# Attention output by half batches, and the first context tokens prepared in the last self-attention batch

## The chip, the cores and the metric

The program runs on one core of one Trainium2 chip. The core has five engines with a queue of instructions each, worked off in order: TensorE (PE, with weight loads shown apart as PEld), VectorE (DVE), ScalarE (ACT), GpSimd (POOL) and SyncE (SP, here used for issuing DMA transfers). The engines wait for each other by semaphores. The metric is the device time of one execution in microseconds (us); lower is better. A profile is one execution taken by the hardware profiler; its span is the time from the first to the last instruction.

## The reference, cut to what matters

Four transformer blocks are chained over x of shape (4, 1024, 288), with a context of (4, 64, 288). Blocks 0 and 3 (`L0`, `L3`) are the same network with different weights, and the change concerns these two:

```python
h = layer_norm(x, ln1_g, ln1_b, 1e-06)
q8, s, sm = quant_act(h)           # rounded to -127..127, one scale per token
q, k, v = (quant_linear(q8, s, sm, w, b) for w, b in ...)      # 8-bit weights
a = attn(q, k, v)                  # 16 heads of 18, 1024 x 1024
a8, sa, sma = quant_act(a)
x = x + quant_linear(a8, sa, sma, wo1, bo1)
h = layer_norm(x, ln2_g, ln2_b, 1e-05)
q8, s, sm = quant_act(h)
q = quant_linear(q8, s, sm, wq2, bq2)
a = attn(q, cond @ wk2.T + bk2, cond @ wv2.T + bv2, mask)      # 64 context tokens
a8, sa, sma = quant_act(a)
x = x + quant_linear(a8, sa, sma, wo2, bo2)
h = quant_linear(quant_act(layer_norm(x, ln3_g, ln3_b, 1e-05)), wfc1, bfc1)
return x + quant_linear(quant_act(gelu(h)), wfc2, bfc2)        # 288 -> 1152 -> 288
```

Block 1 (`L1`, called vip in the kernel) is a cross-attention with two sets of keys, without norm or rounding; block 2 (`L2`) is another quantised transformer block. In blocks 0 and 3 only self-attention mixes the tokens of x, and only those of one batch: every other step can be taken for a few tokens by themselves as soon as their x is there.

## The kernel before, in words

x stays in SBUF for the whole program as 32 tiles of 128 tokens by 288 channels, eight tiles (`NTB`) to each of the four batches (`B`). The 16 heads are taken in four groups (`NG`). Block 0 and block 3 are each one call of `quant_net`; block 0's call also weaves block 1 into its last stage; block 2 is another function, which the change does not touch.

`quant_net` first calls `quant_self`, the self-attention. Its main loop runs over batch, head group, half of the queries (512 tokens) and key tile: 256 steps, each with four score products (line 2021), two exponentials (line 2031) and, one step behind, four products of exponentials and values (`weigh`, line 1981). All other work is woven in by `step()`, called once per loop step: it takes one piece (one `yield` of a Python generator) from the list `side`, in whose generators the operands of the next head group and the norms, roundings and values of the next batch stand, and if `side` is empty one from `spare`, which prepares the 8-bit weights of the later stages in 85 pieces and stores them in HBM. When the eight query halves and groups of a batch are done, `turn_heads` divides by the softmax sums (`heads_done`, lines 1936 to 1954) and appends `output(b)` to `side`: it rounds two tiles at a time (`round_levels`, lines 1414 to 1422), turns them (`turn_levels`, lines 1434 and 1437), multiplies them by wo1 and adds the result to x (`level_residual`: product in line 277, then lines 1755 and 1757 on DVE and line 1758 on POOL). For the last batch all of this comes after the loop: the last `weigh`, the rest of `spare`, then what is in `side`.

After that `quant_net` lays out SBUF and PSUM anew for the stage that follows. `ctx_stage` gives eight generators of four tiles each, the context attention: norm of x (`norm_apply`: line 1401 on ACT, 1404 and 1405 on POOL), rounding (`levels`: lines 1324 to 1333, turned in line 1349, copied in line 1354), the scales of the tokens spread over all partitions (`scale_cols`, line 2346; `over_tokens`, product in line 2358, copy in line 2363), query product (line 2212), attention, wo2 and its bias (line 1762). `ff_stage` gives 32 generators of one tile, the feed-forward. In block 0 `vip_aside` makes block 1's keys and values (loads in lines 2521 and 2527, products in line 2536, memsets in line 2567) and `vip_tokens` applies them. `run_stages` is a planner: from figures of cost that each generator yields it fixes the order in which the pieces are issued; a scheduler then orders each engine's queue and puts in the waits. Instructions of one engine are never overtaken at run time, and a transfer is issued on SP's or POOL's queue, in order, and waits there for its memory to be free. `tc.tile_pool` gives rotating buffers: with `bufs=1` the next tile of the same tag waits until all readers of the last one are done.

## Time and profile before

| | us |
|---|---|
| median of 3 runs | 4948.09 (4947.86 to 4956.46) |
| profiled execution | 4945.58 |
| its span | 4943.8 |
| PE busy in the span | 4245.7 (86%) |
| ACT busy | 3092.6 (63%) |
| DVE busy | 2986.6 (60%) |
| POOL busy | 1292.3 (26%) |
| last attention product of block 0 ends | at 785.5 |
| first context query product of block 0 starts | at 834.5 |
| last attention product of block 3 ends | at 4468.1 |
| first context query product of block 3 starts | at 4527.2 |

Busy time is the sum over an engine's instructions; the shares of different engines overlap. "Granted clock" is the share of TensorE's full rate that the chip's throttle allowed; its mean over this span was 0.848. A row `DVE amx L1324 <- POOL h L1405` among the waits says that DVE's instruction of line 1324, which writes amx, waited for POOL's of line 1405, which writes h.

### The profile page before, as it was taken

The numbers are of one execution on the slowest core, as the hardware profiler recorded it, in microseconds if no ns is written. First come the engines' busy times: TensorE is split into PE (matmuls) and PEld (weight loads), VectorE is DVE, ScalarE is ACT, GpSimd is POOL, SyncE is SP. The second block draws the span as 40 slices with busy tenths as digits, with TensorE's granted clock in tenths as the row PEclk, the third lists the DMA queues.
The fourth block names the chain that finished last, engine by engine and source line by source line (L and its number), as shares of the span: only waits on it lengthen the run. The fifth ranks groups of instructions, "written<-read, shape, count | busy, mean of one in ns | idle before, by whom it ended". The sixth has DMA issues, their size and how long they took to land. (4 is left out here: it accounts for less than half of the span.)

```text
span 4943.8 us, 63809 instructions
## 1 busy us (share of the span) xinstructions
PE 4245.7 (86%) x23291; PEld 1727.7 (35%) x23291; DVE 2986.6 (60%) x6645; ACT 3092.6 (63%) x4379; POOL 1292.3 (26%) x1934
## 2 busy tenths in 40 slices
PE   4999997888899979998888863899998999996676
PEld 2233323455565411110233331445543333322343
DVE  8454254665564589999788878433235455344775
ACT  3776774666662279998888853212114777774796
POOL 1001003443312576420112224111111010004664
PEclk9999998898999955555698885899998999997898
DMA  2000003100001221000000022001000000011000
GB/s 82 4 5 15 15 19 87 47 5 17 3 13 44 114 67 36 26 6 0 22 27 25 22 95 77 24 7 34 1 1 16 7 4 12 16 22 34 12 17 21
DMA packets 137702, 135.99 MB, mean 28 GB/s; under 512 B 69276, under 2 KB 114973, under 8 KB 135713
## 3 DMA queue, kind: packets, MB, share of 16 engines
q1 hardware_dynamic: 136176, 128.13, 8.6%
q0 software_dynamic: 1200, 3.69, 0.3%
q8 instruction: 185, 3.03, 0.3%
q14 instruction: 141, 1.15, 0.1%
HBM read 79.92 MB, written 43.47 MB: 25 GB/s over the span
## 5 line engine op out<-in xcount | busy, mean ns | idle before, releaser
L2031 ACT ACTIVATE e<-ps 128x1024 f32<-128x1024 f32 x1024 | 992.6, 1021 | 381.4 <-PE ps L2021 370.2
L2021 PE MATMUL ps<-qT,kT 32*128 32x512 f32 x4096 | 624.0, 644 | 4.1 <-DVE a L1943 3.9
L3025 DVE TENSOR_REDUCE top<-e 128x2 f32<-128x2048 f32 x256 | 563.5, 2274 | 14.2 <-ACT e L3018 14.0
L1981 PE MATMUL ps<-e,v 128*32 128x512 f32 x4096 | 549.4, 607 | 12.5 <-DVE oT L1992 12.5
L3394 PE MATMUL ps<-qk 32*128 32x512 bf16 x1024 | 499.9, 604 | 40.7 <-ACT e L3018 38.9
L3443 ACT ACTIVATE e<-ps 128x1024 f32<-128x1024 f32 x512 | 483.6, 1055 | 76.9 <-PE ps L3434 58.5
L3018 ACT ACTIVATE e<-ps 128x1024 f32<-128x1024 f32 x512 | 520.5, 1153 | 6.7 <-PE ps L3394 3.3
L1758 POOL TENSOR_TENSOR x<-x,y 128x288 f32<-128x288 f32 x192 | 153.2, 809 | 832.1 <-DVE y L1757 491.2
L3446 DVE TENSOR_SCALAR eb<-e 128x2048 bf16<-128x2048 f32 x256 | 321.7, 1260 | 47.7 <-ACT e L3443 45.5
L1404 POOL TENSOR_TENSOR h<-h,g 128x288 f32<-128x288 f32 x176 | 141.5, 808 | 507.2 <-ACT h L1401 474.5
L3434 PE MATMUL ps<-qk,kz 64*128 64x512 bf16 x1024 | 229.5, 445 | 41.9 <-ACT e L3443 37.8
L2021 PEld LDWEIGHTS ps<-qT,kT 32*128 32x128 f32 x4096 | 188.2, 184 | 208.4 <-issue 118.6
L2463 PE MATMUL psf<-hT,w 128*128 128x512 f32 x576 | 257.8, 600 | 0.6 <-ACT hT L2455 0.6
L1981 PEld LDWEIGHTS ps<-e,v 128*32 128x32 f32 x4096 | 81.0, 108 | 406.5 <-issue 347.1
L1349 PE MATMUL ps<-idb,q 128*128 128x128 bf16 (+2 forms) x1152 | 113.1, 243 | 126.3 <-ACT q L1333 72.7
L3394 PEld LDWEIGHTS <-qk 32*128 32x128 bf16 x1024 | 53.0, 99 | 465.1 <-issue 464.2
L3343 ACT ACTIVATE gl<-psf,bf 128x512 f32<-128x512 f32 x72 | 46.0, 684 | 269.0 <-PE psf L2467 264.8
L1354 ACT COPY qT<-ps 98x384 bf16<-98x384 bf16 (+3 forms) x256 | 151.7, 642 | 72.2 <-PE ps L1349 72.0
L277 PEld LDWEIGHTS <-qT 98*128 98x128 bf16 (+2 forms) x1344 | 134.6, 104 | 128.0 <-issue 41.3
L3347 DVE SCALAR_TENSOR_TENSOR u<-psf,bf,gl 128x512 f32<-128x512 f32 x72 | 51.1, 746 | 211.9 <-ACT gl L3343 211.9
L1880 POOL TENSOR_TENSOR v<-y,wv1b 128x288 f32<-128x288 f32 x64 | 51.7, 813 | 476.6 <-DVE y L1877 476.6
L3018 ACT ACTIVATION_READ_ACCUMULATOR e<-ps 128x1 f32 x512 | 172.9, 338 | 0.0
(506 smaller groups left out, 7803.0 us busy)
## 6 DMA issues: line engine op xcount, KB each, us to landing
raw<-y SPq DMA_DIRECT2D x32, 432.0 KB
in<-raw SPq DMA_DIRECT2D x30, 432.0 KB
kz<-qk SPq DMA_DIRECT2D x128, 64.0 KB
wn<-in_L_wfc SPq DMA_DIRECT2D x12, 432.0 KB
x<-in_x SPq DMA_DIRECT2D x4, 1152.0 KB
vvo<-vt SPq DMA_DIRECT2D x16, 288.0 KB
vo<-vvo SPq DMA_DIRECT2D x4, 1152.0 KB
rawq<-y SPq DMA_DIRECT2D x32, 144.0 KB
```

Source lines behind the costliest of these rows:

```text
L1354: nc.scalar.copy(qT[:, c0 : c0 + r, j0 * P : (j0 + per) * P].rearrange("p c (a t) -> p a c t", a=per), ps[:width, : per * r * P].rearrange ...
L1758: nc.gpsimd.tensor_tensor(self.x[:, t, :], self.x[:, t, :], y, ALU.add)
L1981: nc.tensor.matmul(acc[i * HP : (i + 1) * HP, :], lhsT=st["v"][:, kt, h * (D + 1) : h * (D + 1) + HP], rhs=es_[i // 2][:, i % 2, :], start ...
L2021: nc.tensor.matmul(pss[i // 2][:, i % 2, :], lhsT=self.row_tile(kT, i)[:, kt * P : (kt + 1) * P], rhs=self.row_tile(qT, i)[:, qh * 512 : ( ...
L2031: nc.scalar.activation(e, ps, AF.Exp, scale=SCALE)
L2463: nc.tensor.matmul(o, lhsT=lhs(i)[:, c, :], rhs=rhs(i)[:, c, :], start=(c == 0), stop=False)
L3018: nc.scalar.activation(e[:, j, :].rearrange("p (a n) -> p a n", a=2), sc, AF.Exp, scale=rstep, accum_out=sums[:, t, h0 + j : h0 + j + 1],)
L3025: nc.vector.tensor_reduce(top[:, t, h0 : h0 + 2], e, AX.X, ALU.max)
L3394: self.last = self.nc.tensor.matmul(ps[:, c, :], lhsT=self.row_tile(qT, i)[:, g, qt * P : (qt + 1) * P], rhs=self.row_tile(kT, i)[:, g, c ...
L3434: nc.tensor.matmul(pss[i][:, n, :], lhsT=kz[rows, i, kt * P : (kt + 1) * P], rhs=qT[rows, g, qh * 512 : (qh + 1) * 512], start=True, stop= ...
L3443: nc.scalar.activation(e[:, 2 * n : 2 * n + 2, :], ps, AF.Exp, scale=step)
L3446: nc.vector.tensor_scalar(eb, e, MAGIC, MAGIC, ALU.add, ALU.subtract)
```

## The change

- The output of self-attention is made in two halves of four tiles. The first half is appended to `side` as soon as the first query half of the last head group is done, the second after the other. The attention result `a` is now two tiles of a pool of its own (`halves`).
- A new generator `early` is appended to `side` during the last batch. It takes the norm statistics of batches 0 and 1 for the context stage, and normalises, rounds and turns the first four tiles into a buffer that outlives self-attention (`hT0`), with their scales (`srep0`). The norm uses DVE for all three operations (`norm_dve`), the scale columns too. The generator of the first context tokens takes these as they are.
- ln2's gain and bias (`g2`, `b2`) are loaded ahead of self-attention's.
- The pools of the last stage are laid in another order; context attention and feed-forward get separate work pools, so separate buffers of the same tag (`y`, two each). Fewer buffers are given to the rounded values `q` (x: 2; y: one less, and at most 4), to `oT` and `aT` (1), to the feed-forward's `h` (at most 5) and to `t` in `vip_aside` (1). In `vip_tokens` xT becomes a part of qT.

The diff, cut to its core:

```diff
         nc.vector.reciprocal(rs, sc)
-        q = self.wk.tile([P, m, n + terms], BF16, tag=f"q{tag}", name="q", bufs=bufs)
+        qb = {"x": 2, "y": max(2, min(bufs - 1, 4))}.get(tag, bufs)
+        q = self.wk.tile([P, m, n + terms], BF16, tag=f"q{tag}", name="q", bufs=qb)
...
+    def norm_stats_slow(self, t0, m, eps):
...
             nc.vector.bn_aggr(mv[:, j, :], st[:, j, :])
+            if j % 4 == 3:
+                yield
...
         return rstd, nmr
+
+    def norm_dve(self, h, t, stats, j, g, beta):
+
+        nc = self.nc
+        rstd, nmr = stats
+        nc.vector.tensor_scalar(
+            h, self.x[:, t, :], rstd[:, j : j + 1], nmr[:, j : j + 1], ALU.mult, ALU.add
+        )
+        nc.vector.tensor_tensor(h, h, g, ALU.mult)
+        nc.vector.tensor_tensor(h, h, beta, ALU.add)
...
         self.mm(ps[:, :C], qT[:, :, j * P : (j + 1) * P], w["T"], 0, C)
-        y = self.tmp(C, "y")
+        y = self.wk.tile([P, C], F32, tag="y", name="y", bufs=2)
...
             pool = lambda name, bufs: es.enter_context(tc.tile_pool(name=name, bufs=bufs))
-            wp, at = pool(f"{L}aw", 1), pool(f"{L}at", 2)
+            wp = pool(f"{L}aw", 1)
...
                     wo = self.level_weight(wp, np_, [(w["wo1"], w["bo1"])], C, CK, "wo1")
-            ep = pool(f"{L}ep", 5)
+            halves = pool(f"{L}ah", 3)
             es.enter_context(self.work(f"{L}ak"))
+            at, ep = pool(f"{L}at", 2), pool(f"{L}ep", 5)
...
-            def output(b):
-                a = state[b]["a"]
+            def output(b, hf):
+                a = state[b]["a"][hf]
                 now = None
-                for j in range(0, NTB + 2, 2):
+                for j in range(0, 4 + 2, 2):
                     ahead = None
-                    if j < NTB:
+                    if j < 4:
                         ahead = self.round_levels(a[:, j : j + 2, :], "o")
                     if now:
                         q, sc = now
-                        aT = self.wk.tile([CK, NC3, 2 * P], BF16, tag="qTo", name="aT")
+                        aT = self.wk.tile([CK, NC3, 2 * P], BF16, tag="qTo", name="aT", bufs=1)
                         self.turn_levels(q, CK, aT)
                     yield
                     if now:
                         for n in range(2):
-                            self.level_residual(aT, sc, wo, b * NTB + j - 2 + n, n, wo["b"])
+                            t = b * NTB + hf * 4 + j - 2 + n
+                            self.level_residual(aT, sc, wo, t, n, wo["b"])
                             yield
                     now = ahead
-                del state[b]
...
                 nc.vector.tensor_tensor(
-                    state[b]["a"][:, qh * 4 : qh * 4 + 4, g * 72 : (g + 1) * 72].rearrange(
+                    state[b]["a"][qh][:, :, g * 72 : (g + 1) * 72].rearrange(
...
                 if kt == NTB - 1:
-                    o = self.tmp(512, "oT")
+                    o = self.wk.tile([P, 512], F32, tag="oT", name="oT", bufs=1)
                     nc.vector.tensor_copy(o, acc)
                     done.append((b, g, qh, o))
             def turn_heads():
                 b, g, qh, o = done.pop()
                 heads_done(b, g, qh, o)
-                if (g, qh) == (NG - 1, 1):
-                    side.append(output(b))
+                if g == NG - 1:
+                    side.append(output(b, qh))
             run(levels(0))
             run(operands(0, 0))
             run(values(0))
             for b in range(B):
-                state[b]["a"] = at.tile([P, NTB, C], F32, tag="a", name="a")
+                state[b]["a"] = [
+                    halves.tile([P, 4, C], F32, tag="a", name="a") for _ in range(2)
+                ]
...
                         side.append(values(b + 1))
+                    elif g == 1:
+                        side.append(early())
...
-            self.quant_self(L, w, beside, ready)
+            g2 = self.load_bc(wp, w["ln2_g"], C, "g2")
+            b2 = self.load_bc(wp, w["ln2_b"], C, "b2")
+            made = {
+                "hT": wp.tile([CK, NC3, 512], BF16, name="hT0"),
+                "srep": wp.tile([P, 512], F32, name="srep0"),
+            }
+
+            def early():
+
+                for b in range(2):
+                    made[b] = yield from self.norm_stats_slow(b * NTB, NTB, 1e-5)
+                qs = []
+                for k in range(2):
+                    h = self.wk.tile([P, 2, C], F32, tag="h", name="h")
+                    for n in range(2):
+                        t = 2 * k + n
+                        self.norm_dve(h[:, n, :], t, made[0], t, g2, b2)
+                    yield
+                    qs.append(self.round_levels(h, "i"))
+                    yield
+                for k, (q, sc) in enumerate(qs):
+                    cols = slice(k * 2 * P, (k + 1) * 2 * P)
+                    self.turn_levels(q, CK, made["hT"][:, :, cols])
+                    scols = self.scale_cols(sc)
+                    yield
+                    self.over_tokens(sc, made["srep"][:, cols], scols)
+                    yield
+
+            self.quant_self(L, w, beside, ready, early)
             fp = pool(f"{L}fw")
-            g2 = self.load_bc(fp, w["ln2_g"], C, "g2")
-            b2 = self.load_bc(fp, w["ln2_b"], C, "b2")
             for k, v in (("sw", cw["swo"]), ("b", w["bo2"])):
                 cw["wo"][k] = fp.tile([P, C], F32, name=f"wo2{k}")
                 nc.sync.dma_start(cw["wo"][k], v.partition_broadcast(P))
             nb, m, nf = (2, 1, 3) if vip else (3, 1, 6)
-            cp = pool(f"{L}cb")
-            ctx = self.ctx_stage(cw, g2, b2, cp, nb)
-            first = next(ctx)
             g3 = self.load_bc(fp, w["ln3_g"], C, "g3")
             b3 = self.load_bc(fp, w["ln3_b"], C, "b3")
             w1 = self.stored_weight(fp, fw["T1"], fw["sw1"], None, "wfc1")
             w2 = self.stored_weight(fp, fw["T2"], fw["sw2"], w["bfc2"], "wfc2")
             rext = fp.tile([P, 2, 2 * B], F32, name="rext")
             tops = fp.tile([P, NT], F32, name="tops")
-            ctx_gens = [first] + [next(ctx) for _ in range(2 * B - 1)]
             cw["ext"] = rext
+            es.enter_context(self.work(f"{L}rf", 1))
+            ff_work = self.wk
             ff_gens = self.ff_stage(g3, b3, w1, w2, tops, out, m, nf)
-            stages = [
-                (ff_gens, nf, lambda i, d: i * m // 4 in d[1], None),
-                (ctx_gens, nb, lambda i, d: True, None),
-            ]
...
                 }
-                self.pb = pool(f"{L}pq", 4, space=PSUM)
+            cp = pool(f"{L}cb")
+            self.pb = pb = pool(f"{L}pq", 4 if vip else 8, space=PSUM)
+            stages = [
+                (ff_gens, nf, lambda i, d: i * m // 4 in d[1], lambda: (pb, ff_work)),
+                (list(self.ctx_stage(cw, g2, b2, cp, nb, made)), nb, lambda i, d: True, None),
+            ]
+            if vip:
                 vb = pool(f"{L}pv", 4, space=PSUM)
-                es.enter_context(self.work(f"{L}rk"))
+            es.enter_context(self.work(f"{L}rk"))
+            if vip:
...
                 ]
-            else:
-                self.pb = pool(f"{L}p", 8, space=PSUM)
-                es.enter_context(self.work(f"{L}rk"))
...
-    def ctx_stage(self, cw, g2, b2, pool, nb):
+    def ctx_stage(self, cw, g2, b2, pool, nb, made):
         nc = self.nc
         wq, wo, kb = cw["wq"], cw["wo"], cw["kb"]
-        keys, stats, there = {}, {}, {}
+        keys, there = {}, {0: 0, 1: 0}
+        stats = {b: made[b] for b in there}
...
             t0 = b * NTB + hf * 4
-            if hf == 0:
+            if hf == 0 and b not in there:
                 stats[b] = self.norm_stats(b, 1e-5)
                 there[b] = yield "d8.5", None, SIDE
             while b not in there:
                 yield "x1", None, SIDE
-            h = self.wk.tile([P, 4, C], F32, tag="h", name="h", bufs=nb)
-            for j in range(4):
-                self.norm_apply(h[:, j, :], t0 + j, stats[b], g2, b2)
-                if j % 2:
-                    yield "a1.1&g3.2", 0 if j == 1 else None, SIDE
-            hT, sc = yield from self.levels(h, None, CK, "x", 0, nb, SIDE)
-            srep = self.wk.tile([P, 512], F32, tag="srep", name="srep", bufs=nb)
-            for j in (0, 2):
-                two = sc[:, j : j + 2]
-                cols = self.scale_cols(two, nc.gpsimd)
-                yield "g.9", None
-                self.over_tokens(two, srep[:, j * P : (j + 2) * P], cols)
-                yield "p.5&a.4", 0 if j == 0 else None, SIDE
+            if t0 == 0:
+                hT, srep = made["hT"], made["srep"]
+            else:
+                h = self.wk.tile([P, 4, C], F32, tag="h", name="h", bufs=nb)
+                for j in range(4):
+                    self.norm_apply(h[:, j, :], t0 + j, stats[b], g2, b2)
+                    if j % 2:
+                        yield "a1.1&g3.2", 0 if j == 1 else None, SIDE
+                hT, sc = yield from self.levels(h, None, CK, "x", 0, nb, SIDE)
+                srep = self.wk.tile([P, 512], F32, tag="srep", name="srep", bufs=nb)
+                for j in (0, 2):
+                    two = sc[:, j : j + 2]
+                    cols = self.scale_cols(two, nc.gpsimd)
+                    yield "g.9", None
+                    self.over_tokens(two, srep[:, j * P : (j + 2) * P], cols)
+                    yield "p.5&a.4", 0 if j == 0 else None, SIDE
...
                 yield "x1", None, SIDE
-            h = self.wk.tile([P, m, C], F32, tag="fh", name="h", bufs=nb)
+            h = self.wk.tile([P, m, C], F32, tag="fh", name="h", bufs=min(nb, 5))
...
                 ahead = loads(g + 1)
-            ts = [np_.tile([P, B, 2 * T], F32, tag=f"t{n}", name=f"t{n}") for n in range(3)]
+            ts = [
+                np_.tile([P, B, 2 * T], F32, tag=f"t{n}", name=f"t{n}", bufs=1) for n in range(3)
+            ]
...
         b, n, w = t0 // NTB, t0 // 2, 2 * P
-        xT = self.wk.tile([P, 3, w], F32, tag="xT", name="xT")
+        qT = self.wk.tile([P, NG, w], F32, tag="qT", name="qT")
+        xT = qT[:, :3, :]
         for j in range(2):
             self.width_T(xT[:, :, j * P : (j + 1) * P], x[:, t0 + j, :])
             yield "p.9 a.5", 0 if j == 0 else None
-        qT = self.wk.tile([P, NG, w], F32, tag="qT", name="qT")
...
                 )
-        r = xT[:, 0, :]
+        r = qT[:, 0, :]
         nc.vector.reciprocal(r, ps)
         yield "p.9 d1.8", None
         pss = [self.ps1() for _ in range(4)]
```

More of the change, by code (lines that the diff above doesn't have):

```diff
@@ L1369, in norm_stats_of @@
     def norm_stats_of(self, t0, m, eps):
+        try:
+            at = self.norm_stats_slow(t0, m, eps)
+            while True:
+                next(at)
+        except StopIteration as end:
+            return end.value
+    def norm_stats_slow(self, t0, m, eps):
         nc = self.nc
@@ L1773, in psum_attn, with quant_self @@
             yield
-    def quant_self(self, L, w, beside, ready):
+    def quant_self(self, L, w, beside, ready, early):
         tc, nc = self.tc, self.nc
@@ L1835, in norms @@
                             continue
-                        j = 2 * k + n
-                        nc.vector.tensor_scalar(
-                            hn, self.x[:, t, :], stats[0][:, j : j + 1], stats[1][:, j : j + 1],
-                            ALU.mult, ALU.add,
-                        )
-                        nc.vector.tensor_tensor(hn, hn, g1, ALU.mult)
-                        nc.vector.tensor_tensor(hn, hn, b1, ALU.add)
+                        self.norm_dve(hn, t, stats, 2 * k + n, g1, b1)
                 for k in range(2):
```

## The prediction

> **What bounds the kernel now.** I read four views: busy time by stretches of the span, the timeline around the end of self-attention, the waits in that stretch, and the costliest groups. First the stretches, for block 0 and then block 3: the loop of self-attention, the gap from its last attention matmul to the first context query product (line 2212), and the stage of context attention and feed-forward. Columns: stretch, its length, busy us of PE, PEld, DVE, ACT, POOL, granted clock, DMA share, GB/s.
>
> ```profile
> 85.00:785.50 700.50, 684.07 (x4947) 210.59 (x4947) 322.99 (x956) 514.59 (x548) 57.63 (x107) 0.99 0.04 11
> 785.50:834.50 49.00, 14.59 (x87) 9.86 (x88) 25.82 (x60) 14.72 (x27) 36.70 (x59) 0.58 0.48 133
> 834.50:1570.00 735.50, 645.12 (x3941) 407.19 (x3940) 427.65 (x1307) 423.46 (x711) 231.35 (x427) 0.91 0.07 21
> 3768.80:4468.10 699.30, 685.40 (x4947) 210.72 (x4948) 318.43 (x908) 514.78 (x548) 57.09 (x106) 0.99 0.04 11
> 4468.10:4527.20 59.10, 18.75 (x103) 12.93 (x102) 29.75 (x61) 19.84 (x37) 42.60 (x58) 0.54 0.20 62
> 4527.20:4940.00 412.80, 302.81 (x1746) 162.82 (x1744) 279.99 (x985) 309.13 (x493) 221.83 (x403) 0.85 0.05 16
> ```
>
> In both loops PE is busy for 98% of the time: they are bound by TensorE, and DVE (46%), ACT (73%) and POOL (8%) have room. In the two gaps, 49.0 and 59.1 us, PE works for 14.6 and 18.8 us. They are latency: one chain of small operations through all engines. Block 0's is seen here in order of time (start, duration, engine; in brackets the idle time before and its releaser):
>
> ```profile
> 782.51 2.98 PE L1981 MATMUL ps<-e,v 128*32 128x512 f32 x16
> 800.72 1.69 POOL L1758 TENSOR_TENSOR x<-x,y 128x288 f32<-128x288 f32 x2 [1.51 <-DVE y L1757]
> 802.44 1.15 ACT L1401 ACTIVATE h<-x,nmr,rstd 128x288 f32<-128x288 f32 x2 [4.46 <-POOL x L1758]
> 810.24 1.53 POOL L1404 TENSOR_TENSOR h<-h,g 128x288 f32<-128x288 f32 x2 [2.90 <-DMA g<-in_L_ln_g]
> 816.30 1.35 DVE L1324 TENSOR_REDUCE amx<-h 128x4 f32<-128x1152 f32 x1 [13.22 <-POOL h L1405]
> 829.79 0.80 PE L2358 MATMUL ps<-idf,scol 128*128 128x128 f32 x2 [4.95 <-POOL scol L2346]
> 834.49 0.63 PE L2212 MATMUL ps<-qT,wq2T 96*128 96x512 bf16 x1
> ```
>
> The last attention matmul ends at 785.5; the eight tiles of the last batch's output reach x by 802.4; then x of the first batch, complete long ago, is normalised (ACT, POOL), rounded, turned and scaled, and only at 834.5 does the first query product start. The gain 2.9 us before 810.24 is a wait for the gain's load. The waits of the two gaps (waiting, releaser: total, times, longest) say the same of both blocks:
>
> ```profile
> PE ps L1349 <- ACT q L1333: 16.7, 3, 16.2
> DVE amx L1324 <- POOL h L1405: 13.9, 2, 13.2
> PE ps L2358 <- POOL scol L2346: 7.9, 3, 4.9
> ```
>
> ```profile
> PEld L1349 <- POOL h L1405: 21.1, 1, 21.1
> DVE amx L1324 <- POOL h L1405: 20.7, 3, 15.5
> PE ps L1349 <- POOL h L1405: 20.6, 1, 20.6
> ```
>
> **Removed: the chain of the first context tokens, from both gaps.** Its input is ready during the loop, and `early()` does it there, so after the change the first query product stands on PE directly behind the last output product. The gap shrinks to the tail of the output. Of that the first half (four tiles) also goes into the loop, but the rest is a chain: copy and turn of the last heads (785.5 to 787.8 before), then two pairs of tiles, which before reached x 3.1 to 4.4 us apart (787.8 is followed by a rounding of some 2.8 us, a turn, a copy and products of 3 us, and a second pair 4.1 us later). That is about 12 us.
>
> **Added to that tail: weight preparation.** Counting the 256 steps of the loop, the side work used 159 and left 97 for the 85 pieces of weight preparation; with early (12 pieces) and more output it leaves 76, so 9 pieces, part of wfc2, come after the loop: 5 roundings of 0.406 and 7 copies of 0.308 on DVE, 4.2 us, which is where the tail's chain also runs, and their stores. Tail: 12 + 4.2 = 16 to 17; I take 16.5.
>
> **Moved into the loop.** PE is full there, so its share is paid in full: transposes of two pairs (0.54 each) and four output products (0.45) for the output half, 2.9; two turns (0.54) and two scale spreads (0.66) for early, 2.4; less seven groups of weight transposes (0.3) that leave, 2.1: +3.2 us a block. On DVE early brings 16 statistics of 0.62, 12 norm operations of 0.45, two roundings of about 2.2 and the scale columns (no row on DVE: between 0.1, the least operation here, and POOL's 0.60 each; I take 0.6, four of them), 22 us, and the output half 7 us; the cover is DVE's 377 idle us in the loop, and without it all 29 would be paid. ACT gets four copies of 0.8 and two of 0.37, 3.9 us, against 186 idle; POOL four x updates of 0.81.
>
> Here a rule speaks against the change. DVE's two-input sums (line 1757) took 0.82 for two with POOL idle and 0.81 for two at 796.59, with POOL's selects running: no slowing. The Trainium skill, "SBUF — State Buffer", section "Who interferes with whom", says that a DVE operation with two SBUF inputs and a GpSimd operation that reads SBUF shut each other out for the whole instruction. By the row the eight new sums of g2 and b2 cost 8 x 0.45; by the rule each may also wait for a POOL operation of up to 0.81, 6.5 us in all. DVE has 377 us to lose: nothing on the path either way.
>
> **Block 0's sum.** 49.0 - 16.5 - 3.2 = 29.3 us earlier. Not all of it lasts: the vip products (line 2536), which PE did from 834.9 to 856.6 directly after the first query product, now stand in PE's order behind a few steps of the first context tokens and need Wk and ctx from HBM. SP issues those behind the last weight stores. First query product at 785.5 + 3.2 + 16.5 = 805.2, stores landed about 807.5, two ctx loads at 1.5 us an issue (six took 8.89), landing some 5 us on in a busy queue (DMA share 0.83 to 0.95 from 800 to 820): about 816 instead of 834.9, a gain of 19. PE would idle for 11 us less what it can do of the first tokens, whose steps took 856.6 to 872 before; I take 5 us of that. Gain 29.3 - 11 + 5 = 23, range 15 (loads land at 820) to 29 (all filled). By the clock a pause can cost more: PE's granted clock was 0.50 over 800 to 820 and "TensorE: Matmul & The Clock Gate", section "Part 1: The HAM clock gate", has the array at half rate after an idle window of 3.4 us and as long again to recover, so a second pause makes this 1.7 us less; before, the row shows one cold stretch for the whole gap and none charged twice. I keep 23.
>
> **Block 3's sum.** 59.1 - 16.5 - 3.2 = 39.4. No vip loads here, but the second tokens (0,1) keep the old chain. They start behind the stores (about 4490), and need POOL norms 8 x 0.8, rounding 6, turn and scale 10: ready about 4513, where before their query product came at 4543.6: 31 earlier. Between the two values I take 33, range 26 to 39.
>
> **Smaller items.** Block 3's start: the loads of g2 and b2 now stand on POOL's queue ahead of g1 (issues of 0.58 and 0.54; POOL waited 2.2 us for g1 there): +1, 0 to 2. In block 0 the norm waits for other loads that landed long before: 0. Fewer buffers (rounded values, oT, aT, vip's t, the feed-forward's h in block 3) and vip's xT inside qT: unseen in any row. Nothing, if each is free again before its next use; the worst that I can name is POOL's queue, where the memset of t waits for the store of the group before, with scale columns and x updates of the first tokens behind it: four groups of up to 4 us. I take +2, 0 to 16. Separate y buffers for context and feed-forward could give some back: 0 to -5, taken as 0. The statistics of batches 0 and 1 leave the stage (DVE, 58% busy there): 0.
>
> **Sum:** -23 - 33 + 1 + 2 = -53 against the profiled 4945.58 (span 4943.8 plus 1.8 around it): 4892.6. The median is 2.5 above that execution; the same shift gives 4948.1 - 53 = **4895**.
>
> **Rivals.**
> (A) A larger gain, 4873. In the stages PE idles for 90 and 110 us; with both halves and the feed-forward earlier, and work buffers of their own, some 22 of these 200 go too. For it: the first feed-forward product came only at 923.8 and 4599.8. Against: the planner's order ends with the same work.
> (B) Half is eaten, 4923: loads land at 820 or later in block 0 (gain 10), in block 3 the stores hold ACT and POOL back to a gain of 20, buffers cost 5. For: both blocks put stores ahead of the loads on SP.
> (C) Slower, 4962: fewer buffers. Where the feed-forward or a rounding waits for its buffer, each of 32 tiles a block pays. The point from which it decides: 56 us gained in the gaps over 64 tiles is 0.9 us a tile; at 1.1 us a tile, 70 us, it is slower than before. Against: one piece of two or three rounding buffers is read for about 2 us (four turns of 0.8), much less than a tile's 23 or 13 us of stage.
> (D) No gain: the stages are bound by throughput, so that what starts earlier ends at the same time. Needs PE, or another engine, full; PE at 88 and 73% denies it. 4945.
>
> **How the numbers follow.** Chances: forecast 0.57, A 0.13, B 0.18, C 0.07, D 0.05. The forecast's own range: -15 to -29, -26 to -39, 0 to 2, and 0 to 8 of the 16 give 4880 to 4917. The whole range leaves out C, D and the far end of A: 4864 to 4930. A measurement of this kernel tells 0.2%, 10 us, from no change; faster is forecast, A and B, 0.88; D is within, 0.05; C slower, 0.07.
>
> **What would show it.** Right: gaps of about 17 us to the first query product in both blocks; loops 3 us longer with DVE near 50%; no L1404 or L1405 before line 2212; stages of unchanged length, block 0's some 6 us longer. Wrong: L2536 waiting for ctx beyond 820; POOL's memset of line 2567 idle before for several us; feed-forward or rounding lines of DVE and ACT with new waits for PE's turns; a tail over 25 us; or a stage longer by what the gap lost.

## The result, and the profile after

The changed kernel takes 4932.62 us (median of 5 runs, 4926.36 to 4935.42) against 4948.39 before (5 runs, 4947.86 to 4956.46): ratio 0.9961, 95% interval 0.9947 to 0.9976. It is faster by 16 us, or 0.4%. 53 were forecast (4895, range 4864 to 4930), so the sign was right and the size was not.

Busy time by stretches in the profile of the changed kernel, with the columns of before. For block 0 and then block 3: the loop, the gap to the first context query product (now line 2261), and what follows it.

```profile
86.60:806.30 719.70, 696.13 (x4969) 214.89 (x4968) 337.99 (x1009) 518.14 (x554) 58.98 (x109) 0.98 0.04 10
806.30:830.10 23.80, 8.75 (x54) 5.44 (x54) 22.36 (x57) 4.30 (x7) 15.64 (x27) 0.60 0.36 97
830.10:1561.00 730.90, 642.50 (x3960) 399.40 (x3959) 419.20 (x1281) 414.29 (x708) 244.74 (x445) 0.92 0.10 29
3765.90:4483.10 717.20, 695.31 (x4965) 213.94 (x4963) 325.33 (x932) 517.43 (x554) 58.81 (x108) 0.98 0.04 10
4483.10:4501.20 18.10, 8.29 (x53) 5.13 (x52) 12.83 (x45) 3.96 (x7) 3.93 (x6) 0.61 0.24 58
4501.20:4930.00 428.80, 310.31 (x1772) 164.23 (x1771) 294.94 (x1001) 316.17 (x509) 248.87 (x440) 0.84 0.07 22
```

The gaps shrank from 49.0 and 59.1 to 23.8 and 18.1 us, where 16.5 was forecast for both. But the loops grew from 700.5 and 699.3 to 719.7 and 717.2, by 18 to 19 where 3.2 was forecast.

All comparisons below use four stretches that can be cut alike in every profile. Loop: from the first to the last copy of `oT`. Rest of block 0: from there to block 2's first exponential. Rest of block 3: from the end of its loop to the end of the span. What lies outside (the starts of blocks 0 and 3, and block 2) holds next to none of the change, and took between 2155.6 and 2170.1 us in the 14 profiles of this study. A total from one profile is uncertain by that much, and the four stretches are a better witness. They come from one profile each; the five kernels whose loops hold the same work (before, e7, e9, e11, e12) differ by up to 2.9 us in a loop, so a difference of 2 or 3 us in one stretch says little by itself.

| kernel | loop 0 | rest 0 | loop 3 | rest 3 | sum | median us | ratio to before (95%) |
|---|---|---|---|---|---|---|---|
| before | 665.0 | 981.0 | 666.5 | 475.7 | 2788.2 | 4948 | 1 |
| changed | 682.0 | 951.3 | 684.6 | 450.6 | 2768.4 | 4932.62 | 0.9961 (0.9947 to 0.9976) |
| e1, no early | 680.5 | 965.6 | 684.8 | 460.9 | 2791.8 | 4963.88 | 1.0037 (1.0024 to 1.0050) |
| e2, whole outputs | 667.7 | 949.1 | 669.1 | 442.5 | 2728.4 | 4891.94 | 0.9890 (0.9873 to 0.9906) |
| e3, halves in last batch | 672.5 | 950.4 | 674.4 | 450.2 | 2747.4 | 4902.66 | 0.9904 (0.9888 to 0.9921) |
| e4, turns later | 668.1 | 944.9 | 667.8 | 449.9 | 2730.8 | 4891.92 | 0.9884 (0.9868 to 0.9901) |
| e5, e4 and nothing left over | 670.3 | 952.0 | 670.9 | 440.6 | 2733.8 | 4892.57 | 0.9880 (0.9864 to 0.9897) |
| e6, nothing left over | 684.5 | 946.2 | 683.6 | 435.1 | 2749.5 | 4907.32 | 0.9913 (0.9896 to 0.9931) |
| e7, pools only | 665.7 | 972.7 | 665.0 | 467.1 | 2770.5 | 4930.92 | 0.9956 (0.9942 to 0.9970) |
| e8, last batch, later, nothing left | 667.1 | 951.5 | 669.4 | 435.5 | 2723.5 | 4888.67 | 0.9876 (0.9859 to 0.9893) |
| e9, e7 and the wait | 666.0 | 973.5 | 666.5 | 475.1 | 2781.1 | 4944.26 | 0.9987 (0.9980 to 0.9994) |
| e10, e2 and the wait | 668.2 | 956.4 | 668.7 | 443.5 | 2736.9 | 4897.01 | 0.9894 (0.9877 to 0.9910) |
| e11, e7 and two t | 666.6 | 972.2 | 665.8 | 465.7 | 2770.2 | 4930.72 | 0.9959 (0.9946 to 0.9971) |
| e12, e7 with one work pool | 667.9 | 968.2 | 666.8 | 471.7 | 2774.6 | 4937.27 | 0.9963 (0.9949 to 0.9977) |

Where the loop's 17 us come from is seen at the end of the last batch. The timeline of the changed kernel there (start, duration, engine; in brackets the idle time before, and its releaser):

```profile
786.37 1.70 PE L2042 MATMUL ps<-qT,kT 32*128 32x512 f32 x8
...
788.00 1.06 PE L1998 MATMUL ps<-e,v 128*32 128x512 f32 x8
...
788.55 0.41 DVE L1606 TENSOR_SCALAR wn<-wn,wps 96x384 f32<-96x384 f32 x1
788.88 0.25 DVE L1959 RECIPROCAL rc<-ps 128x16 f32<-128x16 f32 x1
...
791.97 0.52 DVE L1444 TENSOR_SCALAR q<-a 128x288 bf16<-128x288 f32 x2
792.33 0.44 PEld L1456 LDWEIGHTS <-q 128*96 128x96 bf16 x6 [4.17 <-DVE q L1444]
792.33 0.58 PE L1456 MATMUL ps<-idb,q 128*96 128x128 bf16 x6 [3.26 <-DVE q L1444]
...
793.98 1.94 PE L1998 MATMUL ps<-e,v 128*32 128x512 f32 x8
```

The turn of the rounded output (line 1456) stands on PE's queue directly behind the loop step in which the softmax sums came. DVE first finishes a piece of weight preparation (line 1606), then divides (line 1959), then rounds (line 1444). PE stands still for 3.26 us; the attention products behind the turn, ready or not, wait too. After that the same eight products of line 1998 take 1.94 us instead of 1.06. The stretches around the pause show why, by the column before the last two (granted clock). They are cut on the grid on which the clock changes (see the last section):

```profile
786.97:790.38 3.41, 2.10 (x16) 0.43 (x12) 3.38 (x18) 1.94 (x2) 0.00 (x0) 1.00 0.17 24
790.38:793.79 3.41, 1.46 (x14) 0.75 (x14) 3.10 (x14) 0.79 (x1) 0.00 (x0) 1.00 0.00 0
793.79:797.20 3.41, 3.41 (x19) 1.00 (x19) 0.42 (x1) 1.94 (x2) 0.00 (x0) 0.50 0.01 2
797.20:800.62 3.42, 3.42 (x31) 0.78 (x27) 1.53 (x4) 1.94 (x2) 0.80 (x1) 1.00 0.00 0
```

The clock falls after the pause, not in it: to 0.50 for 3.41 us of full work, which costs half of that, 1.7 us. In all 14 profiles the low stretches of the loops are at 0.50 and 3.41 us long, or two of them in a row. Each loop of the changed kernel has five, those of before have two and one. Such a turn stands at the end of every batch. PE's waits over the whole loop of block 0 (waiting, releaser: total, times, longest) hold two rows that the profile of before does not have:

```profile
PE ps L1456 <- DVE q L1444: 8.0, 4, 3.3
...
PE ps L277 <- DVE kT L1920: 2.8, 3, 0.9
```

For block 3's loop the parts can be added up by PE's instructions, each counted from the end of the one before: the moved transposes, products and scale spreads take 4.2 us more, attention's own products 6.1 more (four more low stretches cost 6.8 by the clock), and PE's pauses grew from 11.6 to 19.3. That makes 4.2 + 6.1 + 7.7 = 18.0, of 18.1.

### The profile page after: what moved, and what is told of

It reads as the page before. It is cut to its first block, busy times and chain, and to the rows that moved or that the text cites. A ratio compares the mean times of both kernels' runs of the same rounds, so it can differ in the third digit from the quotient of the medians.

```text
span 4933.7 us, 63765 instructions
## 1 busy us (share of the span) xinstructions
PE 4260.1 (86%) x23291; PEld 1717.8 (35%) x23291; DVE 2997.3 (61%) x6691; ACT 3071.3 (62%) x4355; POOL 1273.6 (26%) x1910
## 5 line engine op out<-in xcount | busy, mean ns | idle before, releaser
L1355 ACT COPY qT<-ps 128x640 bf16<-128x640 bf16 (+3 forms) x252 | 149.7, 640 | 81.3 <-PE ps L1350 81.1
```

The costliest lines, as they stand in the source:

```text
L1355: nc.scalar.copy(qT[:, c0 : c0 + r, j0 * P : (j0 + per) * P].rearrange("p c (a t) -> p a c t", a=per), ps[:width, : per * r * P].rearrange ...
```

## The experiments

### What makes the loops long: e1 to e4

Theory A: the halves do, by these pauses. Rival B: the 22 us that early puts on DVE. Rival C: the smaller buffers. Without early (its call and the use of `made` in `tokens` taken out):

```diff
-                    elif g == 1:
-                        side.append(early())
```

> The loops of self-attention, from the first oT copy to the last, are 665 and 666 us before and 682 and 685 after the change. Theory A (pauses): the turns of the first half of each output stand on PE's queue directly behind the last softmax division, before DVE has rounded; PE waits there and its clock falls, and early costs only its own PE work. Then without early the loops are 678 to 682. Theory B: early's work on DVE makes the loops long; then they are near 668. Theory C: the smaller buffers (oT, aT, q) do it; then 679 to 682 as well. In all cases the gap to the first query product goes back to about 45 and 55 us, so the total is some 25 to 45 above the changed kernel by A and C, about 4960 to 4975, and about 4945 by B.

The loops stay at 680.5 and 684.8: B falls. Without early the change is a loss of 15 us, 4963.88 (1.0037). Next, early kept and the halves undone, in the new pools:

```diff
-                if g == NG - 1:
+                if (g, qh) == (NG - 1, 1):
                     side.append(output(b, qh))
```

with `output` running over all eight tiles.

> early stays, the output is made whole again after the second half, with the new pools. Theory A: the loops fall to 667 to 670 (early's PE work and a little), the gaps grow by some 4 to 8 us each, and the total is about 4915. Theory B: loops stay near 680 and the total is above 4935. Theory C: loops stay near 680 as well, since the smaller buffers stay.

The loops fall to 667.7 and 669.1, so C falls too. The total falls further than any theory had said, to 4891.94: this kernel also has no weight preparation left over after the loop (nine pieces in the changed kernel), which e6 takes up. Next, halves in the last batch alone:

```diff
-                if g == NG - 1:
+                if g == NG - 1 and (qh == 1 or b == B - 1):
                     side.append(output(b, qh))
```

> Halves in the last batch alone; batches 0 to 2 make their output whole. Theory A: the pauses of batches 0 to 2 go, some 7 us of each loop, the last one of 3 us at the end of the loop stays; loops 673 to 676, total about 4917. Theory B and C: loops stay within 2 us of 682 and 685, total about 4930.

672.5 and 674.4: about 10 us of each loop were due to batches 0 to 2. The total, 4902.66, is 14 us below the one expected. And last, all halves kept, but two pieces of weight preparation put between the first rounding and its turn:

```diff
                     yield
+                    if hf == 0 and j == 0:
+                        for _ in range(2):
+                            next(spare, None)
+                            yield
```

> Two pieces of weight preparation are put between the first rounding and the first turn of each first half, so the turn stands on PE's queue two steps (4.6 us) later; the same number of pieces stays for after the loop. Theory A: PE's pauses before the turns (1.1, 1.5, 2.2 and 3.3 us in block 0) go and with them part of the lower clock; loops 672 to 676, total about 4917. Theory B and C: no change beyond 2 us a loop.

This is the direct test of A: in the loop the same work, the turn two loop steps later. The loops are 668.1 and 667.8, below the 672 to 676 expected, and the total is 4891.92. Of the 41 us gained, 31 are the loops'. In block 0 PE's waits before the turns (line 1456) fell from 8.0 to 2.7 us; low stretches of the clock are left three in block 0 and none in block 3. The end of block 0's last batch in e4's timeline:

```profile
779.16 1.06 PE L2002 MATMUL ps<-e,v 128*32 128x512 f32 x8
...
784.12 0.52 DVE L1444 TENSOR_SCALAR q<-a 128x288 bf16<-128x288 f32 x2
...
785.28 0.54 PE L1456 MATMUL ps<-idb,q 128*96 128x128 bf16 x6
...
786.81 1.06 PE L2002 MATMUL ps<-e,v 128*32 128x512 f32 x8
```

Both roundings are done before the turn comes up; PE does not wait for it, and the eight products before and behind it take 1.06 us each.

### What is left over after the loop: e5 and e6

Every 25th step of the loop takes one more piece of weight preparation, so that none is left for afterwards: in the changed kernel (e6, nine were left) and in e4 (e5, seven were).

```diff
+            steps = [0]
+
             def step(n=1):
+                steps[0] += 1
+                if steps[0] % 25 == 0:
+                    next(spare, None)
                 while side and n:
```

> The changed kernel with every 25th step taking one more piece of weight preparation: 9 pieces fewer after the loop, the halves' pauses stay (loops about 683 and 686). Theory S: gaps from 24 and 18 to about 18 and 13, block 3's stage from 432 to about 420; total about 4912. Rival (only their DVE time): about 4928.

> The turns two steps later, as in the kernel that had them so, and every 25th step of the loop takes one more piece of weight preparation, so that no piece is left for after the loop (7 were). Theory S: the left pieces lengthen the tail by their DVE time and, by their stores, hold the second tokens' norm back: both gaps 3 to 5 us shorter, block 3's stage from its first query product on 428 to about 418, loops 1 to 2 us longer; total about 4876. Rival: they cost only their time on DVE, 4 us a block less what the loop pays: about 4888. No effect: 4892.

e6 gains 25 us over the changed kernel (4907.32), and block 3's rest falls from 450.6 to 435.1, more than the pieces' own time on DVE. The timeline of the changed kernel behind the end of block 3's loop (4483.1) shows what comes late:

```profile
4484.04 10.92 SPq L1633 DMA_DIRECT2D w2d<-to  x7
...
4494.27 0.30 DVE L1632 COPY to<-ps 128x288 bf16<-128x288 bf16 x1
...
4498.03 0.79 ACT L1459 COPY aT<-ps 96x768 bf16<-96x768 bf16 x1 [2.53 <-PE ps L1456]
4498.73 4.26 ACT L1423 ACTIVATE h<-x,nmr,rstd 128x288 f32<-128x288 f32 x8
```

In e6, whose loop ends at 4472.0, the last row is:

```profile
4472.12 4.25 ACT L1423 ACTIVATE h<-x,nmr,rstd 128x288 f32<-128x288 f32 x8 [1.28 <-issue]
```

The norm of the second tokens starts 15.6 us after the loop in one kernel and 0.1 us in the other. Their first query product comes 50.9 and 39.2 us after it. The start goes with the number of stores left over: with five, six and seven (e3, e4, the changed kernel) block 3's norm starts at 11.2, 13.4 and 15.6 us. What holds it last in the changed kernel is not a store, though. It stands on ACT's queue directly behind the copy of the last turned output (line 1459), which waits for PE, and the five semaphore instructions between the two take 0.04 us each: nothing was waited for there any more. That the stores put the norm at this late place in the order is likely; no run shows it.

Over the eight kernels with early, block 3's rest follows these second tokens, from a start at 39.2 and a rest of 435.1 us (e6) to 52.1 and 450.2 (e3).

In e5 the gain is not there: 4892.57 after 4891.92. Block 3 gains as expected (449.9 to 440.6), but its loop loses 3.1, and block 0's loses 2.2 and its rest 7.1, although its first query product comes 10 us sooner (11.4 us after the loop instead of 21.6). Where block 0's first tokens start is thus not what sets its end. Nor is it the second tokens, which block 3 follows: in e3 they come at 43.7 and the rest is 950.4, in e4 at 45.7 and it is 944.9. What sets it stays open.

e5 and e6 differ from each other in the turns alone, so they test A a second time: loops of 670.3 and 670.9 against 684.5 and 683.6. They also show that the wait before a turn does not measure its cost. In e6 these waits come to 3.7 us in block 0, less than half of the changed kernel's 8.0, and the loop is no shorter: it has seven low stretches of the clock instead of five, and the pieces put in may have a price of their own (by e5 against e4 2.2 and 3.1 us a loop, hardly more than the scatter).

### What the pools did: e7, e9, e11, e12

Neither early nor halves, only the pools, the buffers and the earlier loads of g2 and b2:

> Neither early nor halves: only the new pools, the smaller buffers, separate work pools for context and feed-forward, and the earlier loads of g2 and b2. If the smaller buffers cost time (the forecast's rival C), this is slower than before by 10 us or more, above 4958. Theory: within 5 us of before, 4944 to 4954, with loops of 665 to 667 and gaps of 49 and 59 as before.

Both expectations were wrong: this is 18 us faster than before (0.9956). The smaller buffers cost the loops nothing (665.7 and 665.0); in the stages behind them a cost could only hide under a gain of 8 us in each block. In block 3 the timeline of ACT and POOL tells where that comes from. Before, ACT's first norm of the context tokens starts at 4485.09, 16.9 us after the loop, behind the last x update, though it reads the first batch's x, which had been complete for long. It writes a buffer in memory that self-attention's pools had held, so the likely reason is that this memory was not free before. In e7, with the pools laid anew, whose loop ends at 4471.1, it starts with the loop's end:

```profile
4471.49 0.63 ACT L1423 ACTIVATE h<-x,nmr,rstd 128x288 f32<-128x288 f32 x1 [1.56 <-issue]
```

So e9 puts the wait back, as a data dependence of POOL's half of the norm (ACT's still starts with the loop's end):

```diff
+        z = self.sm.tile([P, 1], F32, tag="g2z", name="g2z", bufs=1)
+        nc.gpsimd.tensor_scalar(z, self.x[:, NT - 1, :1], 0.0, None, ALU.mult)
+        nc.gpsimd.tensor_scalar(g2, g2, z, None, ALU.add)
```

> The pools-only kernel with one wait put back: POOL adds 0 times the last tile of x to ln2's gain, so POOL's norms of the context tokens start only when the last x update of self-attention is done, as they did before the change, where the norm's buffer was freed by it. From the end of the loop to block 2's first exponential, and to the end of the program in block 3, before took 981 and 476 us and pools-only 973 and 467. Theory R: the gain of the pools is this release; then 979 to 983 and 474 to 478, total about 4948. Rival: the gain comes from the separate work pools in the stages; then 973 and 467 stay, total about 4931. Theory L (DVE and POOL keep each other out): in pools-only the tail of the output took 28.7 and 29.3 us with 16 and 24 POOL norm operations beside it, and its roundings on DVE 0.89 instead of 0.30; with the norms behind the tail, it is 17 us again with 0.30. Without L the tail stays at 28.

Block 3's rest goes back to 475.1 (475.7 before): there it was the norm's earlier start. Block 0's stays at 973.5: there it is something else. e12 tries the separate work pools:

```diff
-            es.enter_context(self.work(f"{L}rf", 1))
-            ff_work = self.wk
...
-                (ff_gens, nf, lambda i, d: i * m // 4 in d[1], lambda: (pb, ff_work)),
+                (ff_gens, nf, lambda i, d: i * m // 4 in d[1], None),
```

> The pools-only kernel with context attention and feed-forward in one work pool again, as before the change. From the end of block 0's loop to block 2's first exponential before took 981 us, pools-only 973, pools-only with the wait put back still 973.5; so 8 us of block 0 have another cause. If it is the separate buffers, block 0 goes back to 979 to 983 and the total to about 4939. If it is not (the order in which the pieces and loads are issued, or the gain's and bias's earlier loads), block 0 stays at 971 to 975 and the total at about 4931. In block 3, where the two stages overlap as well, from the end of the loop to the end of the program: 467 by both, unless separate buffers matter there, then 470 or more.

Block 0 takes 968.2, less than expected by either theory: not the separate pools. In block 3 one pool costs 4.6 us, and the reason is again the norm: ACT's first one is back at 16.9 us after the loop's end (4467.1), as before the change.

```profile
4484.02 2.18 ACT L1423 ACTIVATE h<-x,nmr,rstd 128x288 f32<-128x288 f32 x4 [4.46 <-POOL x L1780]
```

So it is the separate work pools that gave the norm a buffer that is free early. In block 0 e12's norm is back at 16.9 us too, and costs nothing there. All of e7, e9 and e12 begin block 1's key products (line 2536 before) at 15 to 27 us after the loop, inside the gap, where before they began at 49.4; the loads of block 1's weights now stand ahead of the feed-forward's on SP. That fits the 8 us, and no run isolates it. The last of the smaller buffers, two of t in e7:

```diff
-                np_.tile([P, B, 2 * T], F32, tag=f"t{n}", name=f"t{n}", bufs=1) for n in range(3)
+                np_.tile([P, B, 2 * T], F32, tag=f"t{n}", name=f"t{n}", bufs=2) for n in range(3)
```

> The pools-only kernel with two buffers of vip's t again. If the wait of POOL's memset for the store of the group before costs time, block 0 from the end of its loop to block 2's first exponential is 5 to 15 us below the 973 of pools-only, total about 4921. If it is hidden (my theory, since PE is at 88% in that stage), within 3 us, total about 4930.

972.2 against 972.7: the wait of POOL's memset is hidden.

### DVE beside POOL in the tail: e9 and e10

e9 also answers the question that the prediction had settled by one row. In e7 the tail of the output, from the end of the loop to the last x update, takes 28.7 and 29.3 us in the two blocks; in e9, with the norms behind it, 19.5 and 18.0; before, 16.9 in both. Block 3's tail in e7 (POOL adds norms, DVE rounds and adds the bias):

```profile
4482.93 0.95 POOL L1427 TENSOR_TENSOR h<-h,b 128x288 f32<-128x288 f32 x1
4483.85 0.85 POOL L1426 TENSOR_TENSOR h<-h,g 128x288 f32<-128x288 f32 x1
...
4483.97 2.01 DVE L1779 TENSOR_TENSOR y<-y,wo1b 128x288 f32<-128x288 f32 x2
...
4488.40 1.11 DVE L1444 TENSOR_SCALAR q<-a 128x288 bf16<-128x288 f32 x2
```

and in e9:

```profile
4477.15 0.52 DVE L1444 TENSOR_SCALAR q<-a 128x288 bf16<-128x288 f32 x2
4477.59 0.82 DVE L1779 TENSOR_TENSOR y<-y,wo1b 128x288 f32<-128x288 f32 x2
```

Single instructions: a rounding takes 0.30 alone and 0.89 beside a norm, a bias sum 0.45 and up to 1.04. A second cause lies in the same rows: the x updates are POOL's, and in e7 they stand among the norms on its queue. e9 takes both away at once, so the shares are not known. The same wait in e2 asks whether that decides anything once early is there:

> The same wait put into the kernel with early and whole outputs. The norms that it holds back are those of the second tokens (and third in block 3); the first are made early. Theory L: the tails shrink from 23 and 25 to about 17 us, the first query product comes 5 to 7 us sooner after the loop, the second tokens come at about the same time as without the wait, total 4885 to 4892. Without L: tails unchanged and the second tokens some 10 us later, total about 4905.

The tails are 18.2 and 16.9 us instead of 23.0 and 24.8, and the first query products 15.7 and 14.8 us after the loop instead of 23.2 and 22.7. Yet the total is 4897.01 (4893.03 to 4903.83), no better than e2's 4891.94 (4887.55 to 4897.21). The second tokens, whose norms had to wait, come at 48.4 and 45.8 instead of 47.9 and 43.4. So a tail shorter by 5 and 8 us gained nothing; why block 0's rest is even 7 us longer is not shown.

### A faster version: e8

Halves in the last batch alone, its turn two steps later as in e4, and every 25th step with one more piece, as in e6.

> Halves in the last batch alone, with its first turn two steps later, and no piece of weight preparation left for after the loop. By theories A and S together: loops 668 to 670, gaps about 18 and 13, block 3's stage about 419; total about 4875, the same within 5 us as with halves in all batches and both repairs. If halves in batches 0 to 2 still cost something once they are turned later, this is the faster by 5 us or more.

4888.67, ratio 0.9876: 61 us faster than before and 44 us faster than the changed kernel, though 14 us above the time expected; as in e5, block 0's rest did not fall. It is 3 us below e2, which has no halves at all, and the ranges of their runs overlap (4884.33 to 4893.87 and 4887.55 to 4897.21). The halves, repaired, are worth at most a few us; early and the pools are the change's gain. What early does by itself is seen in e2 against e7: the rests fall by 23.6 and 24.6 us, the loops grow by 2.0 and 4.1, and the total falls by 39.

## Why the prediction was wrong

**The moved work in the loop (+3.2 us a block) is the step that failed.** It measured +17.0 and +18.1. The prediction's "PE is full there, so its share is paid in full" counted PE's own work, which is 4.2 us in block 3 and nearly right. It did not ask at which place of PE's in-order queue the turn stands and whether its input is ready there, and it put nothing for the clock in the loop, though it weighed that cost for the gap. In block 3 PE's longer pauses took 7.7 us in place of nothing, and attention's products at the lower clock 6.1; without such turns (e2, e4) the loops are within 1 to 3 us of before. The two loops make 28.7 us of the missing 37. DVE's 377 idle us were no cover: half of an engine's time is free on average, and the rounding that PE waited for was still behind another piece.

**The pieces left over** were counted rightly, nine, and costed at their time on DVE, 4.2 us a block. In block 3 taking them away gained 15.5 (450.6 to 435.1), because with them the second tokens' norm starts 15.6 us after the loop and not with its end. The prediction had block 3's second tokens ready 42 us after the loop (4513 less 4468.1 and 3.2); they came at 50.9, and at 39.2 with nothing left over.

**The gaps** shrank by the mechanism that was forecast, to 18.1 in block 3 and to 23.8 in block 0, 7 more than the 16.5. Block 0's rest fell by 29.7, where 23 + 3.2 = 26.2 was forecast, and block 3's by 25.1 for 36.2. In both, 8 to 9 us come from the pools (e7), which the forecast did not have, so the near agreement in block 0 is partly luck. In block 3 the left-over pieces are more than the missing 11: without them (e6) the rest falls by 40.6.

**The pools** were taken at a loss of 2 and gained 18 us by themselves. The prediction showed ACT's row of line 1401 with `[4.46 <-POOL x L1758]` and called the input "complete long ago", but did not ask why ACT then waited for the last x update. e7 and e12 show that the laying of the pools decides that start. Rival C, slower by fewer buffers, is refuted by e7, which has them and is faster.

**The start of block 3** (+1) measured nothing: POOL waited 2.16 us for g1's load, 2.22 before.

**The rule weighed against a row.** The prediction let a row decide against the Trainium skill's "SBUF — State Buffer", "Who interferes with whom". The row was the wrong one: POOL's selects of 128x1 beside it. With sums of 128x288 on POOL the runs show what the page says, also for the roundings with one SBUF input, which it names as operations that can take both ports: 0.89 for 0.30. The conclusion "nothing on the path" was about the loop, where POOL is nearly idle, and nothing speaks against it there. In the tail the norms beside it add 5 to 11 us (e10 against e2, e9 against e7), by this and by POOL's own queue together, though by e10 nothing was gained by taking them away.

**The rivals.** The result lies between the forecast and no change, nearest to B in size. B's place was wrong, though: it had loads and stores ahead of the next stage, and the greater part was lost in the loop. The forecast's 53 is close to what e2 gains without halves (57 us), but that is luck: 18 of it are the pools', for which the forecast had a loss of 2.

## What to carry to other kernels

Work that is moved beside a full engine costs more than its own time if it stands on that engine's in-order queue before its input is ready: put two or more steps of other work between producing and using it (e4: 31 us in two loops for moving a turn by two steps). When a row's releaser is not an input of the waiting instruction, look for memory that comes free, and place the next stage's first buffers where nothing late is still in use. Count pieces that no longer fit into a loop by what then starts later, not by their own time.

## What the runs showed of the hardware

In these loops the clock of TensorE goes by windows. In each of the 14 profiles all changes of the granted clock lie on one grid of 3.41 us. Of the windows at full clock in the loops, all 45 with PE busy, by the profile, for less than 47% were followed by a window at 0.50, of the three between 47 and 51% two were, and none of the 30 with 51 to 60%; of some 5400 busier ones 8 were, with nothing to show why. So the place of a pause counts, not its length alone. The pause of 3.26 us above left PE busy for 1.46 us of a window, 43%, and the clock fell. In block 3 of e7 a pause of 3.12 us lies across two windows, which stay busy for 60% and 49%, and the clock held:

```profile
4129.39:4132.80 3.41, 2.04 (x15) 0.52 (x11) 3.27 (x14) 2.53 (x4) 0.57 (x3) 1.00 0.00 0
4132.80:4136.21 3.41, 1.66 (x11) 0.37 (x11) 3.31 (x13) 0.66 (x1) 0.00 (x0) 1.00 0.00 0
4136.21:4139.62 3.41, 3.41 (x27) 1.17 (x26) 1.76 (x4) 1.94 (x2) 0.00 (x0) 1.00 0.02 5
```

The Trainium skill's "TensorE: Matmul & The Clock Gate", section "Part 1: The HAM clock gate", gives a free-running window of about 3.4 us, which agrees, and an idle window before the rate halves; here a window idle for a little over half sufficed. Each low window costs 1.7 us on top of the pause where PE has work for all of it.

DVE slows beside POOL by kind of instruction. In e7's profile DVE's reductions of 128x1152 took 1.34 us with and without a POOL instruction beside them, and sums from PSUM 0.52; roundings from SBUF went from 0.30 to 0.89 (medians of 111 and 17).
